# Opening, gate-weight loads and last output of a four-layer conditioned residual kernel, re-ordered

## The chip, the cores and the metric

The kernel runs on one core of a Trainium2 chip. The core's engines work side by side, each through its own queue in order: TensorE (PE in the profile, with PEld its weight loads), VectorE (DVE), ScalarE (ACT), GpSimd (POOL) and SyncE (SP), which here issues nearly all DMAs. Time is device microseconds of one whole execution, the median of several runs. One further execution was taken with the hardware profiler; its rows are what is read below.

## The reference, cut to what matters

`x` is 16 sequences (batch B) of 512 steps (S) with 512 features (D), all float32; `cond` is one vector of 512 per sequence. Four layers follow one another, each added to its input.

```
# layer 0: a wavelet transform, scaled by a gate and undone: as a whole v + gate * v
gate = sigmoid(silu(cond @ W1.T + b1) @ W2.T + b2)
x1 = x + (x + gate * x)                        # = x * (2 + gate)
# layer 1: a recurrence over the 512 steps, h0 = cond
h[t] = tanh(x1[t] @ Wx + b + h[t-1] @ Wh)
x2 = x1 + h
# layer 2: gates, then sums and products along the sequence
f, i = sigmoid(x2 @ Wf.T + bf), sigmoid(x2 @ Wi.T + bi)
f, i = f / (f + i + eps), i / (f + i + eps)
hidden = scan(f, i * (x2 @ Wh2.T + bh), start=cond)
x3 = x2 + hidden
# layer 3: a weight matrix of its own for each sequence
h3 = gelu(layernorm(cond) @ w1 + b1)
A, C = split(h3 @ w2 + b2)                     # 512 x 8 each, per sequence
out = x3 + x3 + x3 @ (base + A @ C.T)
```

## The kernel before

`P` is 128, `KC` is 4 (chunks of 128 features), `T` is 8 steps in a block, `NBLK` is 64 blocks, `BP` is 32.

**Opening (lines 208 to 297).** SP issues, in this order, `cond`, `condT` (the conditioning with features on partitions), `vecs` (bias vectors), `w1`, `w2`, `x0`, `wx`, `wh`, `x1` and a third block of x. ACT issues four small DMAs that spread the recurrence's bias over the partitions of `bias_sb`. POOL clears tiles, copies `condT` into `h0` (the start of the recurrence) and builds an identity. DVE and ACT normalize `cond` into `xhat`. `turned_layer` (L254) is a small dense layer: 16 products (32 passes of TensorE, since a float32 product takes two) into one PSUM bank, a 32x32 block transpose on DVE, a bias sum and a sigmoid. It runs twice, with `w1` and then `w2`, and yields `g2`, 2 + gate. `gated` (L167) multiplies a quarter of a block of x by `g2`; after the second layer DVE does the four quarters of block 0 and then the four of block 1.

**Recurrence (lines 299 to 577).** PE, ACT, DVE and SP follow the written order (`manual_schedule`). PSUM banks start as the bias (`begin`, L185: [...]ACT copies the bias in). `inputs(n, i, pre)` (L383) adds products of x1 with a chunk of `wx` to a bank; `accumulate` (L373) is the product itself, at L374 for `wx` and `wh` alike. A step then adds h @ Wh (16 products), ACT takes tanh in four pieces (L538), and DVE turns each piece (L539) into the operand of the next step. What else PE does in the wait for tanh is given per step: `inputs` of the next block (`SHARE`), a quarter of a layer of layer 3 (`layer_part`, L320), a quarter of an early gate of layer 2 (`early_gate`, L402, matmul at L421). In block 0, the first four `inputs` come ahead of the loop and those of the next step behind each step's h @ Wh. `end_layer(0)` (L344), at the end of block 0, takes the one Gelu (L358). Sigmoids of `early_gate` (L435) begin in block 4.

`wf`, `wi`, `wc` and `base`, 16 pieces of 256 KB, are loaded two at a time after each block from block 1 on (L563). `load_chunk` (L311) brings layer 3's weights through three buffers, and x comes a block at a time, into one buffer (`load_x`, L150).

**Gates and output (lines 579 to 681).** For each of 16 sequences, `gate_unit` (L588) does the rest of layer 2 for each of four feature chunks, and `last_layer` (L653) the output: for each of four groups of 128 steps, four products over k (L658) into one PSUM tile, a copy on ACT (L662) to `osb`, a tile of the pool `work`, which has two buffers, and a DMA out (L663). For the last sequence this starts when the previous one's is through; chunk 3 of its x3 is the last thing that DVE makes (L630).

```
    pending = None
    for b in range(B):
        ...
            if j == (KC - 1 if end else 1) and pending is not None:
                last_layer(*pending)
        ...
        pending = b, x3, base_sb if end else layer
    last_layer(*pending)
```

Of the kernel before, what the change touches and what calls it, by code (L numbers as in the profile page):

```python
# [70 lines left out]

EPS = 1e-8
# [7 lines left out]
def kernel(  # L80
# [127 lines left out]
    with tc.tile_pool(name="pre", bufs=1, side="right") as pre, tc.tile_pool(  # L208
        name="ps_pre", bufs=1, space=PSUM
    ) as ps_pre:  # L210
# [4 lines left out]
        nc.sync.dma_start(out=condT_sb, in_=chunks(condT))  # L215
        nc.sync.dma_start(out=vec_sb, in_=vecs)
        nc.sync.dma_start(out=w1_sb, in_=chunks(w1T))
        nc.sync.dma_start(out=w2_sb, in_=chunks(w2T))
        x0 = load_x(0, pre, "x0")
        nc.sync.dma_start(out=wx_sb, in_=chunks(wx))  # L220
        nc.sync.dma_start(out=wh_sb, in_=chunks(wh))
        x1 = load_x(1, pre, "x1")
        xb = load_x(2)
        for j in range(KC):
            nc.scalar.dma_start(
                out=bias_sb[j * BP : (j + 1) * BP],
                in_=l1b[:, j * BP : (j + 1) * BP]
                .rearrange("(o c) f -> o c f", o=1)
                .to_broadcast([BP, KC, BP]),
            )  # L230

        blank = pre.tile([P, 2 * P], BF16)
        nc.gpsimd.memset(blank, 0.0)
        nc.gpsimd.memset(h0, 0.0)
        nc.gpsimd.tensor_copy(h0[:, :, B : 2 * B], condT_sb)
        make_identity(nc, ident)
        for tile_ in (aeT, hT3, b2a_raw, *h_out[G - 2 : T - 1]):
            nc.gpsimd.memset(tile_, 0.0)

        stats = pre.tile([B, 6], F32)  # L240
# [11 lines left out]
        banks = [[begin(n, i, blank) for i in range(NBANK)] for n in range(2)]  # L252
# [22 lines left out]
        turned = ps_pre.tile([P, KC, B], F32, tag="ae", name="ae")  # L275

        def turn():
            for k in range(KC):
                nc.tensor.transpose(turned[:, k, :], xhat[:, k * P : (k + 1) * P], ident[:B, :B])

        def scale():
            for k in range(KC):
                nc.vector.tensor_scalar(
                    aeT[:, k, :B], turned[:, k, :], col(C_LNG, k), col(C_LNB, k), ALU.mult, ALU.add
                )

        z, gate = turned_layer(lambda k: h0[:, k, B:], w1_sb, C_L0B1, "hq", turn)
        hq = pre.tile([P, KC, BP], F32)
        nc.vector.tensor_tensor(hq, z, gate, ALU.mult)
        _, gate = turned_layer(lambda k: hq[:, k, :], w2_sb, C_L0B2, "g", scale)  # L290
# [4 lines left out]
        for i in range(len(MOVES)):  # L295
            gated(nc.vector, xs[1], x1, i)
# [443 lines left out]
```

## Time and profile before

| what | value |
|---|---|
| time, median of 3 runs (lowest, highest) | 1635.35 us (1634.92, 1636.69) |
| profiled execution, its own time | 1637.08 us |
| its span, first to last instruction | 1635.3 us |
| granted TensorE clock over the span | 0.999 |
| PE / DVE / ACT / POOL busy | 98% / 69% / 26% / 11% |
| first product of layer 0 (L259) | at 8.08 us |
| first tanh (L538) | at 19.28 us |
| first matmul of `gate_unit` (L594) | at 918.35 us |
| last copy of the output (L662) | at 1631.67 us |

The profile gives for each group of instructions its busy time, the mean duration of one, and the idle time of its engine ahead of it, with the instruction or DMA that ended that idle time. A timeline shows a start, a duration, the engine, the source line, the output and inputs, and in brackets the idle time before. SPq and ACTq are DMA issues of those queues. Matmul ends are modelled, so what counts for PE is the distance from start to start. The span and the time of the profiled execution differ by 1.8 us of launch and end.

### The profile page before, as it was taken

The numbers are of one execution on the slowest core, as the hardware profiler recorded it, in microseconds if no ns is written. First come the engines' busy times: TensorE is split into PE (matmuls) and PEld (weight loads), VectorE is DVE, ScalarE is ACT, GpSimd is POOL, SyncE is SP. The second block draws the span as 40 slices with busy tenths as digits, with TensorE's granted clock in tenths as the row PEclk, the third lists the DMA queues.
The fourth block names the chain that finished last, engine by engine and source line by source line (L and its number), as shares of the span: only waits on it lengthen the run. The fifth ranks groups of instructions, "written<-read, shape, count | busy, mean of one in ns | idle before, by whom it ended". The sixth has DMA issues, their size and how long they took to land.

```text
span 1635.3 us, 67511 instructions
## 1 busy us (share of the span) xinstructions
PE 1609.0 (98%) x29213; PEld 1142.2 (70%) x29213; DVE 1132.4 (69%) x3608; ACT 419.5 (26%) x2478; POOL 172.5 (11%) x144
## 2 busy tenths in 40 slices
PE   7999999999999999999999999999999999999998
PEld 6887888888888888888888655555555555555554
DVE  3445655656565656565655698888888888899886
ACT  3333333333333333333333211111111111111111
POOL 0000000000000000000000032222222222222221
PEclk9999999999999999999999999999999999999999
DMA  5445332111111111111110001111111111101111
GB/s 188 139 133 148 108 109 63 36 37 36 36 36 37 36 36 36 37 37 36 36 36 24 23 26 34 41 42 39 42 39 42 44 44 45 39 30 44 45 37 58
DMA packets 110171, 87.12 MB, mean 53 GB/s; under 512 B 19200, under 2 KB 88352, under 8 KB 109872
## 3 DMA queue, kind: packets, MB, share of 16 engines
q1 hardware_dynamic: 108768, 82.71, 16.8%
q8 instruction: 229, 3.75, 1.0%
q14 instruction: 70, 0.57, 0.1%
q10 hardware_dynamic: 1104, 0.08, 0.0%
HBM read 55.48 MB, written 27.28 MB: 51 GB/s over the span
## 4 chain that ended last, share of the span: by engine, by line
PE 91%; DVE 5%; issue 2%; DMA 1%; ACT 1%; POOL 0%; SPq 0%; DVEq 0%; POOLq 0%; ACTq 0%
PE pre L374 41%; PE po L658 12%; PE pg L421 12%; PE pf L594 8%; PE pi L594 8%; PE pc L594 8%; DVE s L611 1%; PE pl L648 1%; PE pf L334 1%; DVE s L623 1%; DVE s L619 1%; DVE i L622 0%; DMA w_sb<-in_w1T_dram 0%; DMA xb<-in_xT_dram 0%; DVE f L625 0%
## 5 line engine op out<-in xcount | busy, mean ns | idle before, releaser
L374 PEld LDWEIGHTS pre<-wh_sb,h_out 128*32 128x32 f32 x16384 | 461.6, 110 | 152.6 <-DVE h_out L539 148.1
L374 PE MATMUL pre<-wh_sb,h_out 128*32 128x128 f32 x16384 | 553.5, 273 | 5.1 <-DVE h_out L539 2.2
L539 DVE STREAM_TRANSPOSE h_out<-a 128x32 f32<-128x32 f32 x2048 | 264.5, 186 | 358.6 <-ACT a L538 358.0
L538 ACT ACTIVATE a<-pre 128x32 f32<-128x32 f32 x2048 | 238.2, 202 | 586.5 <-PE pre L374 586.5
L374 PE MATMUL pre<-wx_sb,x 128*32 128x128 f32 x8192 | 283.1, 274 | 2.8 <-DVE x L171 2.1
L374 PEld LDWEIGHTS pre<-wx_sb,x 128*32 128x32 f32 x8192 | 235.9, 110 | 4.1 <-issue 4.0
L658 PE MATMUL po<-layer,x 128*128 128x512 f32 x480 | 208.7, 592 | 0.5 <-POOL x L630 0.5
L594 PE MATMUL pf<-x,wf_sb 128*128 128x384 f32 (+2 forms) x512 | 168.9, 473 | 2.3 <-DVE x L544 1.3
L658 PEld LDWEIGHTS po<-layer,x 128*128 128x128 f32 x480 | 91.1, 190 | 111.6 <-issue 106.0
L594 PE MATMUL pc<-x,wc_sb 128*128 128x384 f32 (+2 forms) x512 | 165.3, 466 | 0.0
L594 PE MATMUL pi<-x,wi_sb 128*128 128x384 f32 (+2 forms) x512 | 165.3, 466 | 0.0
L611 DVE RECIPROCAL s<-s 128x384 f32<-128x384 f32 (+1 forms) x64 | 153.7, 2402 | 2.1
L594 PEld LDWEIGHTS pf<-x,wf_sb 128*128 128x128 f32 x512 | 96.7, 192 | 72.7 <-issue 18.5
L629 POOL TENSOR_TENSOR s<-s,f 128x512 f32<-128x512 f32 x63 | 86.4, 1371 | 513.5 <-DVE s L623 513.5
L594 PEld LDWEIGHTS pi<-x,wi_sb 128*128 128x128 f32 x512 | 97.3, 190 | 57.7 <-issue 0.2
L594 PEld LDWEIGHTS pc<-x,wc_sb 128*128 128x128 f32 x512 | 97.3, 190 | 57.6
L544 DVE TENSOR_TENSOR x<-x,h_out 128x128 f32<-128x128 f32 x256 | 101.1, 395 | 18.6
L609 ACT ACTIVATE f<-pf,vec_sb 128x384 f32<-128x384 f32 (+1 forms) x64 | 36.0, 562 | 289.2 <-POOL s L629 164.9
L662 ACT COPY osb<-po 128x512 f32<-128x512 f32 x64 | 37.5, 586 | 265.7 <-DMA out_dram<-osb 115.6
L610 DVE SCALAR_TENSOR_TENSOR s<-f,i 128x384 f32<-128x384 f32 (+1 forms) x64 | 35.1, 548 | 89.9 <-ACT i L609 88.8
L582 POOL MEMSET zero<- 128x1 f32 x1 | 0.1, 99 | 919.7 <-DMA early<-ei 919.7
L630 POOL TENSOR_TENSOR x<-s,x 128x512 f32<-128x512 f32 x63 | 83.2, 1320 | 4.9
(84 smaller groups left out, 1218.9 us busy)
## 6 DMA issues: line engine op xcount, KB each, us to landing
w<-in_l3w_dram SPq DMA_DIRECT2D x68, 256.0 KB
xb<-in_xT_dram SPq DMA_DIRECT2D x64, 256.0 KB
out_dram<-osb SPq DMA_DIRECT2D x64, 256.0 KB
early<-ef SPq DMA_DIRECT2D x19, 256.0 KB
early<-ei SPq DMA_DIRECT2D x19, 256.0 KB
f<-early SPq DMA_DIRECT2D x32, 64.0 KB
i<-early SPq DMA_DIRECT2D x32, 64.0 KB
f<-early SPq DMA_DIRECT2D x16, 96.0 KB
```

The source lines that it names most:

```text
L374: nc.tensor.matmul(pre[PLACE[g][0]][j * BP : (j + 1) * BP, PLACE[g][1], :], lhsT, tile_columns(w, j), start=False, stop=False, skip_group_ ...
L421: nc.tensor.matmul(ps[c * BP : (c + 1) * BP, :].rearrange("p (b t) -> p b t", **shape), w[:, k, j * P + c * BP : j * P + (c + 1) * BP], x2 ...
L538: nc.scalar.activation(a[:, at], pre[bank][:, place, at], AF.Tanh)
L539: nc.vector.transpose(turned[:, c, :], a[:, at])
L544: nc.vector.tensor_tensor(x2[:, :, :, at].rearrange("p k b t -> p k t b"), xs[n][:, :, t0 // 2, :, :], turned.rearrange("p k (t b) -> p k ...
L594: nc.tensor.matmul(p[:, te:], w_sb[:, k, j * P : (j + 1) * P], x2[:, k, b, te:], start=(k == 0), stop=(k == KC - 1),)
L609: nc.scalar.activation(gate[:, new], p[:, new], AF.Sigmoid, bias=col(bias, j))
L611: nc.vector.reciprocal(s[:, new], s[:, new])
L629: engine.tensor_tensor(s, s, f, ALU.add)
L630: engine.tensor_tensor(x3[:, j, :], s, x2[:, j, b, :], ALU.add)
L658: nc.tensor.matmul(po, x3[:, k, at], layer[:, k, :], start=(k == 0), stop=(k == KC - 1))
L662: nc.scalar.copy(osb, po)
```

## The change

Five things change.

1. The opening. `w1` is issued second on SP, right behind `cond`; `vecs` goes to ACT's queue. `condT` no longer feeds `h0`: TensorE turns `cond` (`turn`, four transposes) and DVE copies the result; `condT` itself is loaded later. The bias is loaded as one row of 2 KB; POOL multiplies it with the identity into `bias_rows`, four products with ones spread it over partitions, and ACT copies it to `bias_sb`. `idle_products(n)` issues n products of zeros, 512 columns wide: three at the start, four ahead of the first layer, one ahead of the second. The banks' zero products move from the start to between the two layers. `wh` is loaded ahead of `wx`, each in four pieces.
2. Block 0. The first h @ Wh stands ahead of the first `inputs`, whose two groups now follow it. The four quarters of block 1's gating move from ahead of the loop into steps 0 to 3. The pool `pre` is closed, and `x2` made, after step 3. The load of `b2a` moves from ACT's queue to SP's, and `condT` comes behind it.
3. A one-element sigmoid follows the Gelu in `end_layer(0)`.
4. The gate weights are loaded one piece at a time, after steps 1 and 5 of blocks 0 to 7.
5. The last sequence's output: chunks 0 to 2 of all four groups first, into four PSUM tiles, then chunk 3 of each with its copy and DMA.

In the instruction streams of the two programs, TensorE has eight more idle products, four more transposes and four bias products. In the changed one ACT's table load ahead of the Gelu waits for DVE, and the Gelu itself for POOL; before, the load waited for nothing and the Gelu for DVE. A second table load follows the Gelu, and the one ahead of the first early sigmoid is gone. ACT's last four copies wait for the DMA of two copies earlier, as before.

```diff
+IDLE = (3, 4, 1)
...
         nc.sync.dma_start(out=cond_sb, in_=cond)
-        nc.sync.dma_start(out=condT_sb, in_=chunks(condT))
-        nc.sync.dma_start(out=vec_sb, in_=vecs)
         nc.sync.dma_start(out=w1_sb, in_=chunks(w1T))
+        nc.scalar.dma_start(out=vec_sb, in_=vecs)
+        bias_row = pre.tile([KC, P], F32)
+        nc.scalar.dma_start(out=bias_row, in_=l1b)
         nc.sync.dma_start(out=w2_sb, in_=chunks(w2T))
         x0 = load_x(0, pre, "x0")
-        nc.sync.dma_start(out=wx_sb, in_=chunks(wx))
-        nc.sync.dma_start(out=wh_sb, in_=chunks(wh))
+        for k in range(KC):
+            nc.sync.dma_start(out=wh_sb[:, k, :], in_=wh[k * P : (k + 1) * P, :])
+        for k in range(KC):
+            nc.sync.dma_start(out=wx_sb[:, k, :], in_=wx[k * P : (k + 1) * P, :])
...
-        for j in range(KC):
-            nc.scalar.dma_start(
-                out=bias_sb[j * BP : (j + 1) * BP],
...
-        blank = pre.tile([P, 2 * P], BF16)
+        blank = pre.tile([P, D], BF16)
         nc.gpsimd.memset(blank, 0.0)
+        make_identity(nc, ident)
         nc.gpsimd.memset(h0, 0.0)
-        nc.gpsimd.tensor_copy(h0[:, :, B : 2 * B], condT_sb)
-        make_identity(nc, ident)
+        ones = pre.tile([KC, BP], F32)
+        nc.gpsimd.memset(ones, 1.0)
+        bias_rows = pre.tile([KC, KC, P], F32)
+        nc.gpsimd.tensor_tensor(
+            bias_rows,
+            bias_row.unsqueeze(1).to_broadcast([KC, KC, P]),
+            ident[:KC, :KC].unsqueeze(2).to_broadcast([KC, KC, P]),
+            ALU.mult,
+        )
...
+        def idle_products(n):
+            ps = ps_pre.tile([P, D], F32, tag="pre", name="idle")
+            for _ in range(n):
+                nc.tensor.matmul(ps, blank[:, :P], blank, start=True, stop=True)
+
+        def turn(src, name):
+            turned = ps_pre.tile([P, KC, B], F32, tag="ae", name=name)
+            for k in range(KC):
+                nc.tensor.transpose(turned[:, k, :], src[:, k * P : (k + 1) * P], ident[:B, :B])
+            return turned
+
+        idle_products(IDLE[0])
+        nc.vector.tensor_copy(h0[:, :, B : 2 * B], turn(cond_sb, "cond_turned"))
...
-        banks = [[begin(n, i, blank) for i in range(NBANK)] for n in range(2)]
+        bias_ps = ps_pre.tile([P, KC, BP], F32, tag="ae", name="bias")
+        for j in range(KC):
+            at = slice(j * BP, (j + 1) * BP)
+            nc.tensor.matmul(
+                bias_ps[at], ones, bias_rows[:, :, at], start=True, stop=True, skip_group_check=True
+            )
+        nc.scalar.copy(bias_sb, bias_ps)
...
-        z, gate = turned_layer(lambda k: h0[:, k, B:], w1_sb, C_L0B1, "hq", turn)
+        idle_products(IDLE[1])
+        z, gate = turned_layer(lambda k: h0[:, k, B:], w1_sb, C_L0B1, "hq", turn_xhat)
         hq = pre.tile([P, KC, BP], F32)
         nc.vector.tensor_tensor(hq, z, gate, ALU.mult)
+        banks = [[begin(n, i, blank) for i in range(NBANK)] for n in range(2)]
+        idle_products(IDLE[2])
         _, gate = turned_layer(lambda k: hq[:, k, :], w2_sb, C_L0B2, "g", scale)
...
-        for i in range(len(MOVES)):
-            gated(nc.vector, xs[1], x1, i)
-        nc.scalar.dma_start(out=b2a_raw[:, :, :R], in_=b2a)
...
             nc.scalar.activation(hT3[:, :, :B], z[:, :, :B], AF.Gelu)
+            nc.scalar.activation(z[:, 0, :1], z[:, 0, :1], AF.Sigmoid)
...
     pre, nxt = banks
-    for i in range(KC):
-        inputs(0, i, pre)
     for _ in range(AHEAD):
         load_chunk()
+    nc.sync.dma_start(out=b2a_raw[:, :, :R], in_=b2a)
+    nc.sync.dma_start(out=condT_sb, in_=chunks(condT))
...
             if n == 0 and s < G - 1:
-                for k in range(KC):
-                    inputs(0, (s + 1) * KC + k, pre)
+                for i in range((s + (s > 0)) * KC, (s + 2) * KC):
+                    inputs(0, i, pre)
...
+            if n == 0 and s < G:
+                gated(nc.vector, xs[1], x1, (0, 2, 1, 3)[s])
+            if n == 0 and s == G - 1:
+                opening.close()
+                x2pool = ctx.enter_context(tc.tile_pool(name="x2pool", bufs=1, side="right"))
+                x2 = x2pool.tile([P, KC, B, S], F32)
...
+            if s in (1, 5) and n < 2 * KC:
+                which, k = divmod(2 * n + s // 5, KC)
+                w_sb, w = ((wf_sb, wfT), (wi_sb, wiT), (wc_sb, wcT), (base_sb, base))[which]
+                nc.sync.dma_start(out=w_sb[:, k, :], in_=w[k * P : (k + 1) * P, :])
...
-        for i in (2 * n - 2, 2 * n - 1):
-            if 0 <= i < 4 * KC:
...
-        pending = b, x3, base_sb if end else layer
-    last_layer(*pending)
+        pending = b, x3, layer
+
+    pos = [
+        pool.tile([P, D], F32, tag=tag, name=f"po_{B - 1}_{t}", bufs=2)
+        for t, (pool, tag) in enumerate(((ps_g, "pl"), (ps_g, "pl"), (ps_o, "po"), (ps_o, "po")))
+    ]
+    for t, po in enumerate(pos):
+        output_part(po, t, x3, base_sb, range(KC - 1))
+    for t, po in enumerate(pos):
+        output_part(po, t, x3, base_sb, (KC - 1,))
+        leave(B - 1, t, po)
```

`output_part` issues the products of a group over the chunks it is given, and `leave` the copy to `osb` and the DMA out; together they are the body of the loop of `last_layer`.

## The prediction

> **What bounds the kernel now.** I read the page's busy times first, then the waits, then the chain and the timeline of the places that the diff touches.
>
> ```profile
> PE 1609.0 (98%) x29213; PEld 1142.2 (70%) x29213; DVE 1132.4 (69%) x3608; ACT 419.5 (26%) x2478; POOL 172.5 (11%) x144
> ...
> PEclk9999999999999999999999999999999999999999
> ```
>
> PE is busy 1609 of 1635.3 us, and the change removes no product of it (it adds a few). So what can be won is PE's 26 us of idle time and time in which its products run slowly. PE's waits in the first 60 us, then from 60 to 960 us:
>
> ```profile
> PE ps_hq L259 <- DMA w_sb<-in_w1T_dram: 5.9, 1, 5.9
> PE pre L374 <- DVE x L171: 2.1, 1, 2.1
> PE pre L192 <- POOL blank L233: 1.1, 1, 1.1
> PE ps_g L259 <- DVE hq L289: 0.9, 1, 0.9
> ...
> PE pg L421 <- DMA wc_sb<-in_wcT_dram: 1.7, 1, 1.7
> ```
>
> The opening holds 10 us of the 26, led by w1; one late gate weight holds 1.7 us more. The timeline of PE and of ACT in the opening:
>
> ```profile
> 15.52 1.93 PE L374 MATMUL pre<-wx_sb,x 128*32 128x128 f32 x32 [2.10 <-DVE x L171]
> 17.20 1.96 PE L374 MATMUL pre<-wh_sb,h_out 128*32 128x128 f32 x32
> 18.91 1.96 PE L374 MATMUL pre<-wx_sb,x 128*32 128x128 f32 x32
> 20.61 1.19 PE L374 MATMUL pre<-wh_sb,h_out 128*32 128x128 f32 x32
> ...
> 23.39 1.07 PE L374 MATMUL pre<-wx_sb,x 128*32 128x128 f32 x32
> 24.26 0.96 PE L374 MATMUL pre<-wh_sb,h_out 128*32 128x128 f32 x28
> ...
> 19.28 0.47 ACT L538 ACTIVATE a<-pre 128x32 f32<-128x32 f32 x4 [4.82 <-PE pre L374]
> 21.92 0.47 ACT L538 ACTIVATE a<-pre 128x32 f32<-128x32 f32 x4 [2.18 <-PE pre L374]
> 23.64 0.47 ACT L538 ACTIVATE a<-pre 128x32 f32<-128x32 f32 x4 [1.25 <-PE pre L374]
> ```
>
> From 17.20 to 18.91 32 passes take 1.71 us, 53 ns each; from 23.39 to 24.26 the same 32 take 0.87, 27 ns each. The granted clock reads 1.00 in both, so the slow state shows only in these distances. It ends near 20.7, after 5.2 us of unbroken work; every product of the two small layers ran in it. A step takes 2.64 us slow (19.28 to 21.92), 1.72 fast.
>
> Two places in the recurrence, seen on ACT, and the end, on ACT and PE:
>
> ```profile
> 33.07 1.28 ACT L358 ACT_TABLE_LOAD   x1
> 34.36 0.26 ACT L358 ACTIVATE hT<-got 128x64 f32<-128x64 f32 x1
> 34.52 0.44 ACT L538 ACTIVATE a<-pre 128x32 f32<-128x32 f32 x4
> ...
> 92.74 1.28 ACT L435 ACT_TABLE_LOAD   x1
> 94.04 0.69 ACT L435 ACTIVATE ef<-pg,vec_sb 128x512 f32<-128x512 f32 x1
> 94.62 0.45 ACT L538 ACTIVATE a<-pre 128x32 f32<-128x32 f32 x4
> ...
> 1620.17 11.43 PE L658 MATMUL po<-base_sb,x 128*128 128x512 f32 x26 [0.45 <-DVE x L630]
> 1631.67 0.59 ACT L662 COPY osb<-po 128x512 f32<-128x512 f32 x1 [2.85 <-PE po L658]
> ```
>
> Both table loads stand ahead of a tanh that the next step waits for.
>
> **The change part by part.** Step A, *the opening*, to the tanh of step 1, now at 21.92. Two paths meet there.
>
> The DMA path. Up to the last piece of wx four weights of 1.05 MB, x0 of 0.26 and 0.05 small must come, 4.51 MB. From 4.5 to 19.5 us the windows show 383 GB/s: 11.8 us. When does the flow begin? In before w1 is issued at 2.18 and the full rate starts at 4.5, 2.3 us later, with about 1,200 small packets (condT, the spread bias, vecs) at 57 to 109 GB/s ahead. The last output, with nothing ahead, is issued at 1632.28 and moves data from 1633.1, 0.85 us later. w1 is now issued at 1.18 with fewer than 200 small packets beside it: the flow starts between 2.0 and 3.5; I take 2.4, nearer the empty queue. w1 lands at about 5.5, wx at 14.2 plus 0.3 for the completion (the last output's data ends at 1634.0, SP sees it at 1634.27): 14.5. The later pieces of wx wait on SP for DMAs eight places earlier (w1, w2, x0); those land at 5.5 to 9, more than 2 us before their turn comes, so I cost this at 0; without that cover it is up to 2 us.
>
> The engines' path. Zeros from 1.2; cond lands at 2.58 as before; four transposes take 0.60 (the row of the four of xhat), the copy 0.2. bias_row, ACT's second issue (0.48 each), lands near 3.1 (cond took 1.84); POOL's multiply over 512 elements costs 1.37 by its row in the gate stage, so 4.5; four bias products 0.5; the four zero products, N = 512 at the slow rate, about 0.43 each (estimate, from the 427 ns of the Trainium skill, "TensorE: Matmul & The Clock Gate", Part 1; L658's f32 pass of 512 columns is 0.43 at full rate, two bf16 passes' worth), 1.7. So the first layer starts at 6.8, not at w1's landing. It takes 1.94 slow: 8.75. hq follows 1.46 later in before (10.02 to 11.48), but PE now has four transposes (0.60), 24 blank products (1.05) and one zero product (0.43) in between, 2.1: the second layer starts at 10.8. By then PE has worked without a hole of note since 4.5, 6.3 us, over the 5.2 that were enough: fast, 1.1, to 11.9. The gate and three quarters of gating take 2.08 (13.44 to 15.52): 14.0. The first h @ Wh lies in that wait, hidden while wh lands by 11.7.
>
> So the paths end at 14.5 and 14.0. The last k's wx products need 0.2 and their latency 0.2: first tanh at 14.9, the second one fast step of 1.75 later at 16.65, against 21.92: **5.2 us** gained. From both sides: flow at 2.0 gives 5.7. If PE stays slow throughout, 10.8 + 1.94 + 2.08 + 1.94 is 16.75, the next tanh 2.64 later at 19.4: 2.5 gained.
>
> Step B, *the sigmoid behind the Gelu*, in the hole between blocks 0 and 1. In before the load starts at 33.07, ahead of Gelu's operand (DVE's add at L357 ends at 33.79). In the changed stream the load itself waits for DVE, since the Gelu now waits for POOL: 33.8 to 35.1, Gelu to 35.4, the second load to 36.7, the one-element sigmoid 0.2 (the row of the 16x1 Sqrt): tanh at 36.85, not 34.52. **2.3 us** lost; behind that tanh wait four transposes and all of PE. The Trainium skill speaks against this edit: "ScalarE: Activation LUTs", What ACT_TABLE_LOAD costs, gives 1.28 us of load and about 1.38 of drain for each switch. The rows of before have the 1.28 and no drain: Gelu starts 0.01 us after its load. I take the rows; by the rule the new load costs 1.4 more, which I keep as the end of the range.
>
> Step C, *the first early sigmoid*. Without its load the sigmoid would run from 92.74 to 93.43, before the products of its step end at 93.7, so tanh at 94.62 moves to 93.75: **0.85 us** gained.
>
> Step D, *gate weights sooner*. PE waits at 126.33 for a piece issued at 122.92. Tanh to tanh there is 3.64 us (124.70 to 128.34), 1.75 in the next step: **1.9 us** gained, as that piece is now issued in step 1 of block 5, over ten steps ahead. The issues cost SP 0.45 each; SP's queue spends 15 us of the first 60 waiting for PE, which hides them.
>
> Step E, *the last output*. PE now fills the hole before 1620.17 (0.6 us) with other chunks: its last pass ends at 1630.9, not 1631.6. But the four copies no longer come 3.43 us apart. Chunk 3 of the groups ends at 1628.3, 1629.15, 1630.0 and 1630.9. Copies 1 and 2 end at 1628.95 and 1629.8; a DMA takes 2.0 from issue to SP's seeing it land, and osb has two buffers, so copy 3 waits to 1631.0 and copy 4 for the second DMA, to 1631.85: 0.2 later than 1631.67. **0.2 us** lost; from 0.7 gained (no wait) to 0.5 lost.
>
> Costed at nothing: block 1's gating in steps 0 to 3, four times 0.25 on DVE, which idles 0.9 us and more before each set of transposes (x1 and the third block land at 15.2 and 15.9, as DVE reaches them; up to 0.5 if late); condT and b2a in small packets, about 2 us of DMA time ahead of the x that was issued at 26.42 for use at 35.15.
>
> Sum: 5.2 - 2.3 + 0.85 + 1.9 - 0.2 = 5.45. The profiled execution took 1637.08, 1.7 above the median of 1635.35; I take the gain off the median: 1629.9, said as 1630.0.
>
> **The rivals.** *PE stays slow through the opening.* Zeros come in bursts of 1.3 and 1.7 us with holes of over 1 us while POOL makes the bias. For it: in before PE worked 8.08 to 10.6 and 11.48 to 13.4 and stayed slow. Against it: 6.3 us nearly unbroken. Then A is 2.5, the sum 2.75: 1632.6.
>
> *The hole of step B slows PE again.* PE's filler ends at 34.4 and h comes near 37.3, a hole of 2.9 us. The same page, Why this matters for your kernels, wants no holes over about 3 us. The trace has only one of 1.6 us (at 87.6) after which PE stays fast, so it can't decide. It would cost two or three slow steps, 0.9 each, 1.8 to 2.7: about 1632.2.
>
> *SP falls behind, and the kernel is slower.* A gate weight now stands ahead of each block's x in SP's queue, in blocks 1 to 7. x, issued at 40.49, is first used at 48.70 and takes 2.0 to land, 6.2 us in hand. If queued weights hold it over 7.0 us longer, DVE's queue, and with it the recurrence, loses 0.8 in each of seven blocks, which eats 5.45; at 8 us it is 1.8 a block, 12.6: 1642.5. For it: SP's queue is in order with its waits on earlier DMAs. Against it: the total of bytes in these blocks hardly changes, 256 KB per 7 us.
>
> **How the numbers follow.** The sum as worked out, with one end or other of its terms: 0.62, 1628.4 to 1631.4. Slow PE in the opening: 0.15. The hole: 0.10. Both of these at once, about 1634: 0.05. The slower rival, or a wait like it: 0.08. The instruction-issue stall of 1.6 us at 87.6 may move either way. Range 1628.1 to 1633.8. 0.2%, about what a measurement of this kernel can tell from no change, is 3.3 us: faster takes the likeliest case and part of the two rivals around 1632.4, 0.70; within 0.2% the rest of them, 0.22; slower 0.08.
>
> **What would show it.** First tanh near 14.9, the second 1.75 later; 27 ns a pass in the second layer's products; two table loads between 28 and 32 and a tanh 2.3 us later than the load-free order would give; no load near 90; no wait for wc; the last copies waiting for the output's DMA, the last one about 3.5 us from the end. A first tanh past 16, slow passes after block 0, or DVE waiting for xb would prove me wrong.

## The result and the profile after

The changed kernel took 1634.58 us (median of 14 runs, 1632.68 to 1638.50) beside 1636.74 us for the kernel before in the same comparison (14 runs, 1634.92 to 1639.18): ratio 0.9988, 95% interval 0.9979 to 0.9996. A second comparison (e13 below, 22 runs) gave 1635.37 us, ratio 0.9994, 0.9988 to 1.0001. So the change brings 1 to 2 us, some 0.1%, where 5.4 were forecast: within the 0.2% that counts as no change, and 0.8 us above the range. Its profiled execution took 1635.84 us with a span of 1634.1, against 1637.08 and 1635.3 before.

PE is what the page shows first, now busy 99% instead of 98%, but 4.7 us longer in sum:

```profile
PE 1613.7 (99%) x29233; PEld 1143.2 (70%) x29233; DVE 1133.1 (69%) x3609; ACT 419.9 (26%) x2480; POOL 173.5 (11%) x145
```

The 20 products added (zeros, the turned cond, the bias) take 5.2 us by their rows, so the rest of PE's work is hardly shorter. PE's waits in the first 60 us:

```profile
PE pre L400 <- DVE h_out L565: 2.9, 1, 2.9
...
PE pre L400 <- DVE x L173: 1.0, 1, 1.0
PE ps_hq L287 <- DMA w_sb<-in_w1T_dram: 0.7, 1, 0.7
```

The 5.9 us for w1 have become 0.7. On top stands a wait of 2.9 us for `h_out` (0.6 in the kernel before): the hole behind block 0, a stretch in which PE stands idle while ACT loads two tables. PE in the opening, and the tanhs of ACT:

```profile
7.18 1.94 PE L287 MATMUL ps_hq<-w_sb,h_out 128*32 128x128 f32 x32 [0.72 <-DMA w_sb<-in_w1T_dram]
...
11.22 1.94 PE L287 MATMUL ps_g<-w_sb,hq 128*32 128x128 f32 x32
12.93 1.32 PE L400 MATMUL pre<-wh_sb,h_out 128*32 128x128 f32 x32
15.23 1.95 PE L400 MATMUL pre<-wx_sb,x 128*32 128x128 f32 x64 [0.98 <-DVE x L173]
```

```profile
16.44 0.47 ACT L564 ACTIVATE a<-pre 128x32 f32<-128x32 f32 x4 [2.22 <-PE pre L400]
18.61 0.47 ACT L564 ACTIVATE a<-pre 128x32 f32<-128x32 f32 x4 [1.70 <-PE pre L400]
```

The second layer still takes 1.94 us, 53 ns a pass; only from 13.48, where the record of the clock begins, does PE run at 27. The wx products start when DVE has x ready, at 15.23; for wx itself PE does not wait here. The tanh of step 1 comes at 18.61 instead of 21.92: 3.3 us gained, and a stall of 0.5 in block 0 leaves 2.84 at its last tanh (29.34 against 32.18).

The end of block 0 on ACT, one line of the kernel before and then the changed kernel:

```profile
32.18 0.47 ACT L538 ACTIVATE a<-pre 128x32 f32<-128x32 f32 x4 [1.25 <-PE pre L374]
```

```profile
31.02 1.28 ACT L382 ACT_TABLE_LOAD   x1 [0.81 <-DVE got L381]
32.31 0.26 ACT L382 ACTIVATE hT<-got 128x64 f32<-128x64 f32 x1
32.59 1.28 ACT L384 ACT_TABLE_LOAD   x1
33.88 0.20 ACT L384 ACTIVATE got<-got 128x1 f32<-128x1 f32 x1
33.99 0.44 ACT L564 ACTIVATE a<-pre 128x32 f32<-128x32 f32 x4
...
36.47 0.47 ACT L564 ACTIVATE a<-pre 128x32 f32<-128x32 f32 x4 [1.87 <-PE pre L400]
38.54 0.47 ACT L564 ACTIVATE a<-pre 128x32 f32<-128x32 f32 x4 [1.61 <-PE pre L400]
```

From the last tanh of block 0 to the first of block 1 (the boundary, below) it takes 4.65 us, 2.34 before (32.18 to 34.52): 2.31 lost. The next two steps take 2.48 and 2.07 instead of 1.63 and 1.65, another 1.27 lost. Busy times by stretch (after each engine's count the column PEclk is the granted clock) say why:

```profile
30.00:34.00 4.00, 1.57 (x58) 1.30 (x48) 0.88 (x4) 3.15 (x6) 0.00 (x0) 1.00 0.47 147
34.00:37.40 3.40, 2.93 (x56) 2.67 (x60) 1.33 (x10) 1.06 (x10) 0.00 (x0) 0.50 0.04 10
37.40:41.00 3.60, 3.60 (x132) 3.24 (x128) 1.34 (x10) 1.10 (x9) 0.00 (x0) 1.00 0.47 146
```

The clock is halved for 3.41 us (33.96 to 37.38) right behind the hole; PE gets 56 products done in it, and 132 in the next 3.6 us.

Further on, the first early sigmoid gives 0.42 back, and in block 7 the wait for wc is gone (1.91). A stall of PE's issue at 87.6, 1.6 us in the profile before, does not occur (about 1.9); others of 0.5 to 1.2 us fall on other steps. The last tanh of the recurrence comes 3.76 us earlier (913.32 against 917.08). Of that 1.2 reach the end of the span. ACT at the last output:

```profile
1626.78 0.59 ACT L687 COPY osb<-po 128x512 f32<-128x512 f32 x1 [10.57 <-PE po L692]
1627.64 0.58 ACT L687 COPY osb<-po 128x512 f32<-128x512 f32 x1 [0.27 <-PE po L692]
1629.51 0.58 ACT L687 COPY osb<-po 128x512 f32<-128x512 f32 x1 [1.29 <-DMA out_dram<-osb]
1630.36 0.58 ACT L687 COPY osb<-po 128x512 f32<-128x512 f32 x1 [0.27 <-DMA out_dram<-osb]
```

The first two copies wait for PE, the last two for the output's DMA. And in the gate stage there is one more stretch at half clock. Before had it too, but for 3.41 us (from 1573.92), while it now lasts 6.83 (from 1569.96). Before, then after:

```profile
1566.80:1573.60 6.80, 5.42 (x18) 2.38 (x16) 6.76 (x9) 0.55 (x1) 2.04 (x2) 1.00 0.00 0
1573.60:1580.00 6.40, 6.40 (x18) 4.24 (x18) 6.40 (x10) 0.53 (x2) 0.66 (x1) 0.73 0.13 33
```

```profile
1566.80:1573.60 6.80, 4.92 (x11) 2.43 (x10) 6.76 (x10) 0.00 (x0) 2.69 (x2) 0.73 0.11 31
1573.60:1580.00 6.40, 6.40 (x19) 4.30 (x18) 6.40 (x10) 1.05 (x2) 0.79 (x1) 0.75 0.00 1
```

### The profile page after: what moved, and what is told of

Same layout as the page of the kernel before. It is cut to its first block, busy times and chain, and to the rows that moved or that the text cites. A ratio compares the mean times of both kernels' runs of the same rounds, so it can differ in the third digit from the quotient of the medians.

```text
span 1634.1 us, 67569 instructions
## 1 busy us (share of the span) xinstructions
PE 1613.7 (99%) x29233; PEld 1143.2 (70%) x29233; DVE 1133.1 (69%) x3609; ACT 419.9 (26%) x2480; POOL 173.5 (11%) x145
## 4 chain that ended last, share of the span: by engine, by line
PE 95%; DVE 2%; issue 1%; ACT 0%; DMA 0%; POOL 0%; SPq 0%; ACTq 0%; POOLq 0%; DVEq 0%
PE pre L400 41%; PE po L692 13%; PE pg L447 12%; PE pf L626 9%; PE pi L626 9%; PE pc L626 9%; PE pl L680 1%; PE pf L358 1%; DVE s L643 0%; DVE s L655 0%; DMA w_sb<-in_w1T_dram 0%; DVE s L651 0%; POOL x L662 0%; POOL s L661 0%; DVE h_out L565 0%
## 5 line engine op out<-in xcount | busy, mean ns | idle before, releaser
L687 ACT COPY osb<-po 128x512 f32<-128x512 f32 x64 | 37.5, 585 | 266.7 <-DMA out_dram<-osb 129.2
```

The source lines that it names most:

```text
L687: nc.scalar.copy(osb, po)
```

## The experiments

Each run was compared with runs of the kernel before on the same chip; a ratio below is to that. Nearly all differences are 1 to 4 us, and an interval of the median is 2 to 3 us wide. So the mechanism is read in the traces and the medians only say whether it reaches the end.

**The hole behind block 0.** Theory: the second load costs its own time, and the hole then halves the clock. *e1* is the changed kernel without the sigmoid:

```diff
-            nc.scalar.activation(z[:, 0, :1], z[:, 0, :1], AF.Sigmoid)
```

> The changed kernel without the one-element sigmoid behind the Gelu. Theory (the hole between blocks 0 and 1 lowers PE's clock): the second table load is gone, the first tanh of block 1 comes 1.5 us earlier after the last of block 0 (3.1 instead of 4.65 us), PE's hole shrinks from 2.9 to about 1.4 us, the granted clock stays 1.00 there, and the next two steps take 1.65 and 1.75 us instead of 2.48 and 2.07, 1.2 more. A load returns ahead of the first early sigmoid and costs 0.4 to 0.85. Net 1.9 to 2.3 us faster than the changed kernel: about 1632.5. Rival (the loads alone, the clock falls for another reason): the clock still falls, net 0.7 to 1.1 faster: about 1633.7.

Measured: 1633.98 us, ratio 0.9989 (0.9980 to 0.9997). The boundary takes 3.14 us (4.65 with the sigmoid), PE's hole is 1.4 instead of 2.9 us, and the clock stays at 1.00 through block 1. In the traces the sigmoid costs 1.51 at the boundary and 1.28 behind it, and returns 0.42. The median does not show those 2.4 us (the changed kernel's ratio is 0.9988); the same trace has a fall of the clock in the opening instead (14.93 to 18.34).

*e2* fills the hole with ten products of zeros in the first step of block 1 and leaves all else:

```diff
+            if n == 1 and s == 0:
+                ps = ps_q.tile([P, WIDE], F32, tag="pg", name="hole")
+                for _ in range(10):
+                    nc.tensor.matmul(ps, zeros_b[:, :P], zeros_b, start=True, stop=True)
```

> The changed kernel with ten products of zeros (N = 512) on PE in step 0 of block 1, where it waits for the Gelu, the two loads and the sigmoid. ACT's work there is the same. Theory (idle PE lowers its clock): the hole is under 1 us, the granted clock stays 1.00 there, tanh 0 to tanh 2 of block 1 takes 3.3 us instead of 4.55: 1.2 faster than the changed kernel, about 1633.4. Rival (the clock falls for another reason than PE's idling): it falls all the same, no gain.

Measured: 1634.98 us, ratio 0.9994 (0.9986 to 1.0003). The same stretches as above, of this kernel:

```profile
30.00:34.00 4.00, 3.78 (x69) 2.30 (x66) 0.98 (x5) 3.14 (x5) 0.00 (x0) 1.00 0.50 166
34.00:37.40 3.40, 2.82 (x100) 2.65 (x104) 1.33 (x10) 1.20 (x11) 0.00 (x0) 1.00 0.06 14
```

The boundary still takes 4.66 us, so ACT's wait is untouched; but the clock stays at 1.00, 100 products fit where 56 did, and the two steps are back at full speed (1.27 us). The median does not show it. So in this trace it is the hole that lets the clock fall, and the loads do so only through it. One trace is weak evidence, since the clock does not fall behind every such hole; the table in the point-by-point part counts all of them.

*e14* adds only the sigmoid to the kernel before.

```diff
             nc.scalar.activation(hT3[:, :, :B], z[:, :, :B], AF.Gelu)
+            nc.scalar.activation(z[:, 0, :1], z[:, 0, :1], AF.Sigmoid)
```

> Kernel before with only the one-element sigmoid behind the Gelu. Theory 1 (the wait and the slow steps after it): the tanh after block 0 comes 2.3 us later, the clock falls for one window behind the hole and two or three steps cost 1.3 together, the load near 92.7 is gone and gives 0.4 to 0.85 back: 2.7 to 3.2 us slower than before. Rival (in this kernel PE's filler reaches further into the hole, so no slow window): 1.5 to 1.9 slower, granted clock 1.00 throughout block 1.

Measured: 1636.34 us beside 1636.26, ratio 0.9996 (0.9988 to 1.0004). ACT at the boundary:

```profile
32.73 0.38 ACT L200 COPY pre<-bias_sb 128x256 f32<-128x256 f32 x1
33.12 1.28 ACT L358 ACT_TABLE_LOAD   x1
34.42 0.26 ACT L358 ACTIVATE hT<-got 128x64 f32<-128x64 f32 x1
34.69 1.28 ACT L360 ACT_TABLE_LOAD   x1
35.98 0.20 ACT L360 ACTIVATE got<-got 128x1 f32<-128x1 f32 x1
36.09 0.44 ACT L540 ACTIVATE a<-pre 128x32 f32<-128x32 f32 x4
```

Here the first load starts right behind the copy, with no wait for DVE. The boundary takes 3.86 us (1.51 more), PE's hole is 1.82 us, and the clock stays at 1.00 through block 1. The tanh at the first early sigmoid gains 0.80. The rival was right about the clock; of its 1.5 to 1.9 us about 0.7 are lost in the trace and nothing in the median. The 2.3 us of the changed kernel are thus 1.5 for the sigmoid and 0.8 because the Gelu's load waits for DVE there.

**The opening.** Two theories for the missing part of the gain: PE at half speed in the second layer, or wx landing later than forecast. *e4* puts the banks' zero products, which stand between the two layers, ahead of the first, so that they do not keep PE from the second:

```diff
-IDLE = (3, 4, 1)
+IDLE = (3, 4, 2)
...
         nc.scalar.copy(bias_sb, bias_ps)
+        banks = [[begin(n, i, blank) for i in range(NBANK)] for n in range(2)]
...
-        banks = [[begin(n, i, blank) for i in range(NBANK)] for n in range(2)]
```

> The changed kernel with the banks' zero products and bias copies ahead of the first small layer, not between the two layers, and two zero products instead of one ahead of the second layer. Theory (what stands between the layers on PE delays the second): the second layer starts 0.7 us earlier against the first one's start (3.3 us after it, not 4.04), first tanh 0.5 to 0.7 earlier; if PE gets fast before the second layer, since it works with fewer holes from 4 us on, 0.9 more. About 1633.5, to 1632.9. Rival (DMA sets the first tanh): wx comes last, the first tanh stays at 16.4.

Measured: 1634.83 us, ratio 0.9998 (0.9990 to 1.0006); neither theory nor rival came true, and the profiled execution, at 1639.78 us, was the slowest of its 13. The second layer runs fast at 11.01, but the first tanh comes at 17.85, 1.4 later than in the changed kernel: PE waits 1.46 us for a piece of wx, until 17.10, and the clock is halved from 17.18 on.

*e5* keeps PE busy through the whole opening with more zeros:

```diff
-IDLE = (3, 4, 1)
+IDLE = (3, 6, 1)
...
         nc.vector.tensor_copy(h0[:, :, B : 2 * B], turn(cond_sb, "cond_turned"))
+        idle_products(2)
...
+            if n == 0 and s == 0:
+                ps = ps_q.tile([P, WIDE], F32, tag="pg", name="fill")
+                for _ in range(4):
+                    nc.tensor.matmul(ps, blank[:, :P], blank, start=True, stop=True)
```

> The changed kernel with PE's holes in the opening filled by more products of zeros: two behind the transposes of cond, six instead of four ahead of the first layer, four between the first h @ Wh and the first wx products. Theory 1 (step A fell short because PE was slow in the second layer): that layer runs at 27 ns a pass, x1 of block 0 is ready near 13.5 and the first tanh comes near 14.9, 1.5 us earlier; no fall of the clock before 30 us. Theory 2 (the weights come later than I put it): x1 is ready as early, but PE then waits for wx, and the first tanh stays at 16.0 to 16.5; what the fill saves is only the slow windows that such waits bring, under 1 us. By 1: about 1633.0; by 2: 1634.0.

Measured: 1633.86 us, ratio 0.9993 (0.9984 to 1.0001). PE in its opening:

```profile
7.49 1.08 PE L288 MATMUL ps_hq<-w_sb,h_out 128*32 128x128 f32 x32
...
10.05 1.08 PE L288 MATMUL ps_g<-w_sb,hq 128*32 128x128 f32 x32 [0.25 <-DVE hq L318]
...
15.68 0.43 PE L401 MATMUL pre<-wx_sb,x 128*32 128x128 f32 x8 [0.71 <-DMA wx_sb<-in_wx_dram]
16.35 1.30 PE L401 MATMUL pre<-wx_sb,x 128*32 128x128 f32 x40 [0.25 <-DMA wx_sb<-in_wx_dram]
```

Both layers run at full speed, and the first tanh is no earlier for it: 16.91, as PE waits for wx until 16.35. That speaks for the transfers. *e6* is e5 without w2's transfer:

```diff
-        nc.sync.dma_start(out=w2_sb, in_=chunks(w2T))
...
-        _, gate = turned_layer(lambda k: hq[:, k, :], w2_sb, C_L0B2, "g", scale)
+        _, gate = turned_layer(lambda k: hq[:, k, :], w1_sb, C_L0B2, "g", scale)
```

> The kernel of the opening filled, with w2 left out: it isn't loaded, and the second small layer multiplies by w1. The same instructions on PE, 1.05 MB less in the queue ahead of x0, wh and wx. Theory 2 (DMA sets the first tanh): wx lands 2.7 us earlier (1.05 MB at 383 GB/s) and the first tanh comes 1.5 us or more earlier than with the opening filled alone, to where the path over the gates ends, near 14.5. Theory 1 (PE's rate and the gates set it): no change, under 0.3 us.

Measured: 1633.27 us, ratio 0.9981 (0.9974 to 0.9987). The wait for wx is gone, and the wx products start when DVE has gated x:

```profile
14.34 1.95 PE L399 MATMUL pre<-wx_sb,x 128*32 128x128 f32 x64 [0.22 <-DVE x L173]
```

First tanh at 15.55, 1.36 us earlier than in e5. So with PE at full speed the bytes ahead of wx set the first tanh. From the start of the wx products to the first tanh it takes 1.21 us here, as in the changed kernel (15.23 to 16.44).

*e12* is the opening alone: the changed kernel without the sigmoid and with the gate weights and the last output as before.

> Parts 1 and 2 of the change alone: the changed kernel without the sigmoid behind the Gelu, with the gate weights loaded after the blocks and the last output in its order as before. By the corrected step A the tanh of step 1 comes at 18.6 (3.3 us gained), and the Gelu's table load, which waits for DVE, gives 0.7 back: about 2.6 faster than before, 1633.3. By step A as predicted, 5.2 and 4.5: 1631.4.

Measured: 1633.53 us, ratio 0.9974 (0.9964 to 0.9983). First tanhs at 16.27 and 18.84; the boundary takes 3.14 us, so the load's wait for DVE comes with the opening. The last tanh of block 0 gains 2.41, and the first of block 1 keeps 1.6. The ratio is worth 4.2 us (interval 2.8 to 5.9; the medians differ by 3.6), more than these 1.6 and nearer to the 4.5 of step A as predicted. *e16* below, which adds the weights, gains less.

**Gate weights.** *e8* moves only the loads of the gate weights, in the kernel before.

```diff
+            if s in (1, 5) and n < 2 * KC:
+                which, k = divmod(2 * n + s // 5, KC)
...
-        for i in (2 * n - 2, 2 * n - 1):
-            if 0 <= i < 4 * KC:
```

> The kernel before with the gate weights alone loaded after steps 1 and 5 of blocks 0 to 7. By step D the wait for wc in block 7 is gone and the tanh there come 1.9 to 2.1 us earlier: about 1634 against 1636. Rival (SP's queue falls behind, x late): DVE waits for xb in blocks 1 to 7 and it is slower than before.

Measured: 1634.67 us, ratio 0.9989 (0.9980 to 0.9998). The tanh at (block 7, step 3) gains 1.91 us, DVE does not wait for `xb` between 20 and 160 us (2.4 us before), and the ratio is worth 1.8 us.

*e16* is the opening and the weights, without the sigmoid and with the old last output.

> Changed kernel without the early sigmoid and with the old last output: the new opening and the earlier gate weights alone. Theory 3 (the parts add up): 3.3 to 4.2 from the opening and 1.8 from the weights, 5 to 6 us under the kernel before, near 0.9965 of it. Rival (what the recurrence gains is lost again in the gate stage, where a slow window of TensorE grows from 3.4 to 6.8 us): 3 to 4 us under it, with the last tanh of the recurrence 5 us earlier and the span only 3 to 4 shorter.

Measured: 1632.82 us, ratio 0.9977 (0.9968 to 0.9986), 3.8 us. The rival was right in the main: the last tanh is 5.74 us earlier, the last reciprocal 5.3, the span 4.5. The clock is halved for 6.83 us in the gate stage (3.41 before), and from the last reciprocal to the last copy it takes 22.1 us (21.4 before).

**The last output and its buffers.** Theory: the new order bunches the four copies, and two `osb` buffers make them wait for the DMAs. *e10* is the kernel before with the new order, *e3* the changed kernel with a third buffer; *e7* and *e11* are the kernel before with a third buffer, with the old and the new order.

```diff
-        osb = work.tile([P, D], F32, tag="osb", name=f"osb_{b}_{t}")
+        osb = work.tile([P, D], F32, tag="osb", name=f"osb_{b}_{t}", bufs=3)
```

> The kernel before with the new order of the last output alone. Step E: from PE's first pass of the last sequence to the end of the span 18.4 to 18.7 us, against 18.3 before; copies 3 and 4 wait for DMAs; time as before within 0.5 us. Rival (PE's filled hole counts): 0.7 us faster.

> The changed kernel with three osb buffers instead of two. Theory (the last copies wait for a buffer, step E): copies 3 and 4 of the last sequence follow their products, 0.86 us apart, without a wait for a DMA; the last copy starts 14.0 us after the first pass of the last sequence instead of 15.0, the span ends about 1.0 us earlier: 1633.6. Rival (the four DMAs close together hold each other up): copies early, but the last DMA lands as late as now, under 0.3 gained.

> The kernel before with three osb buffers instead of two, nothing else. With the changed kernel the third buffer took 7.5 us off. If that comes from the gate stage, which both kernels share (the third and fourth copies of each sequence wait for a DMA that stands in SP's queue behind loads that wait for VectorE), it takes about as much off here: 1628.5 to 1630. If it came from the new order of the last output alone, no more than 1 us.

> The same with three osb buffers. Theory (the buffer, not the DMAs, held the new order back): the four last copies follow their products 0.86 us apart and the order is now worth 0.7 to 1.5 us over the kernel before with three buffers (1633.7): about 1632.5. Rival (three buffers and the new order have nothing to do with one another): 1633.7.

Measured: e10 1637.47 us, ratio 1.0001 (0.9992 to 1.0009); e3 1627.14, 0.9954 (0.9941 to 0.9966); e7 1633.69, 0.9988 (0.9979 to 0.9997); e11 1631.55, 0.9971 (0.9960 to 0.9982). With two buffers the order is worth nothing, with three about 2.8 us (0.9971 against 0.9988, though the two intervals overlap). For e7 neither forecast holds: its 2 us lie between the 1 and the 6 or more. For e3 both sides had expected 1 us at most. The last copies of e3:

```profile
1618.85 0.59 ACT L687 COPY osb<-po 128x512 f32<-128x512 f32 x1 [10.57 <-PE po L692]
1619.70 0.59 ACT L687 COPY osb<-po 128x512 f32<-128x512 f32 x1 [0.27 <-PE po L692]
1620.56 0.59 ACT L687 COPY osb<-po 128x512 f32<-128x512 f32 x1 [0.27 <-PE po L692]
1621.57 0.59 ACT L687 COPY osb<-po 128x512 f32<-128x512 f32 x1 [0.42 <-DMA out_dram<-osb]
```

They are 0.86 us apart, the fourth 1.0. From the last reciprocal to the last copy e3 takes 19.1 us, the changed kernel 23.3 and the kernel before 21.4; that is 4.2 us against the changed kernel. Another 3.2 us lie earlier in the gate stage (690.5 us from the last tanh to the last reciprocal against 693.75). ACT's waits there (total, times, longest), first of the changed kernel, then of e3:

```profile
ACT osb L687 <- DMA out_dram<-osb: 129.2, 24, 8.3
```

```profile
ACT osb L687 <- DMA out_dram<-osb: 0.4, 1, 0.4
```

With two buffers ACT stands 129 us before copies whose buffer is still going out, and the activations queue behind. With three it does not, PE's wait of 1.9 us for DVE near 1567 is gone, and the clock does not fall there (nor in e7, e9 and e11):

```profile
1566.80:1573.60 6.80, 6.80 (x27) 4.82 (x26) 6.80 (x11) 1.05 (x2) 0.00 (x0) 1.00 0.02 5
1573.60:1580.00 6.40, 6.40 (x25) 4.42 (x24) 6.33 (x9) 1.05 (x2) 2.67 (x2) 1.00 0.11 32
```

*e15* is the changed kernel with the old order, *e13* the changed kernel once more, on the same chip as e14 and e16.

> Changed kernel with the last output computed in the old order. Theory 2 (the new order costs 1 to 2 us when the slow window before it lasts 6.8 us, as the copies then wait for two output transfers): 1 to 2 us under the changed kernel of this call, last copies 3.4 us apart, from last reciprocal to last copy 21.4 to 22.3 us. Rival (the order is worth nothing with two buffers, as it was when it alone was added to the kernel before): within 0.5 us of the changed kernel.

> The changed kernel once more, beside three kernels that each hold some of its parts, so that all four are compared with the same runs of the kernel before. Theory (the parts add up: opening 3.3 to 4.2 gained, sigmoid 3.0 lost, weights 1.8 gained, last output about nothing): 2 to 3 us under the kernel before. Rival (slow windows of TensorE move by chance from run to run and the first comparison fell badly): 4 us or more under it.

Measured: e15 1634.34 us, ratio 0.9985 (0.9978 to 0.9992); e13 1635.37, 0.9994 (0.9988 to 1.0001). The new order costs about 1 us in the changed kernel, though the two intervals overlap; for e13, 1 us under the kernel before, neither forecast came true. On this one chip the ratios make a row: opening and weights 0.9977, with the sigmoid 0.9985, with the new order too 0.9994; only its two ends are apart beyond their intervals. The traces show when the order costs. From the last reciprocal to the last copy the old order takes 21.4 us when the late half-clock stretch lasts 3.41 us (before, e8, e15) and 22.1 to 22.3 when it lasts 6.83 (e12, e14, e16); the new order takes 21.6 (e2, e5) and 22.6 to 23.3 (after, e1, e4, e6, e10, e13). So it loses 0.2 in the one case, 0.3 to 1.2 in the other.

e13's trace shows one more thing. It is the same program as the changed kernel, and its opening ran otherwise:

```profile
10.20 1.08 PE L287 MATMUL ps_g<-w_sb,hq 128*32 128x128 f32 x32 [0.25 <-DVE hq L317]
...
13.77 0.43 PE L400 MATMUL pre<-wx_sb,x 128*32 128x128 f32 x8 [0.29 <-DMA wx_sb<-in_wx_dram]
15.79 3.53 PE L400 MATMUL pre<-wx_sb,x 128*32 128x128 f32 x56 [1.59 <-DMA wx_sb<-in_wx_dram]
```

PE was fast at 10.2, stood 1.59 us for wx, and the clock was halved from 15.07 to 21.90: tanhs at 17.73 and 21.15, and 0.3 us gained at the end of block 0, where the first profile had 2.84. It then passed the hole behind block 0 with the clock at 1.00. So from one execution to the next the half-clock stretches sit in different places.

**The best version.** *e9* is the changed kernel without the sigmoid, with three `osb` buffers, and with `hT3` cleared by DVE instead of POOL, so that the Gelu's load does not wait:

```diff
+        nc.vector.memset(hT3, 0.0)
-        for tile_ in (aeT, hT3, b2a_raw, *h_out[G - 2 : T - 1]):
+        for tile_ in (aeT, b2a_raw, *h_out[G - 2 : T - 1]):
```

> The changed kernel without the sigmoid behind the Gelu, with DVE clearing the Gelu's output tile in place of POOL (so that the table load needn't wait), and with three osb buffers. Theory: tanh 0 of block 1 comes 2.3 us after the last of block 0 as in the kernel before, PE's hole is under 1 us, its clock keeps up there; with the 7.5 us of the third buffer and 2.3 + 1.3 - 0.5 from the hole: about 1624.5. Rival (the third buffer's 7.5 was chance of few runs): 1629 or more.

Measured: 1627.47 us, ratio 0.9944 (0.9930 to 0.9958), about 9 us under the kernel before. The boundary takes 2.36 us and the clock is at 1.00 from 12.9 to 1620.6. It beats both kernels; from e3 (0.9954) the intervals do not separate it. It lies between the theory's 1624.5 and the rival's 1629.

## Why the prediction was wrong, point by point

The step that failed is step A, the size of the gain in the opening: 5.2 us were forecast, and 2.4 to 2.8 were left at the end of block 0, because both of the paths that were to end at 14.5 and 14.0 us ended more than 1 us later. The second miss, 1.27 us, is a fall of the clock that the sum left out as an unlikely rival.

- **Step A, 5.2 us forecast: 3.3 at the tanh of step 1, 2.4 to 2.8 at the end of block 0** (after and six other profiles with this opening: e1, e2, e3, e12, e15, e16), 0.3 in e13. The DMA path was sized with full rate from 2.4 and wx landed at 14.5. The stretches of the changed kernel (last column: GB/s) show the start:

```profile
1.50:2.50 1.00, 1.00 (x3) 0.15 (x1) 0.00 (x0) 0.71 (x1) 0.59 (x4) 1.00 0.41 72
2.50:3.50 1.00, 0.81 (x5) 0.50 (x4) 0.08 (x1) 0.57 (x1) 0.59 (x1) 1.00 0.80 195
3.50:4.50 1.00, 0.51 (x8) 0.20 (x8) 0.93 (x4) 0.00 (x0) 1.00 (x5) 1.00 0.97 328
4.50:5.50 1.00, 1.00 (x7) 0.38 (x4) 0.70 (x3) 0.83 (x3) 0.72 (x4) 1.00 1.00 342
```

  The rate climbs from 1.5 to 4.0 us rather than starting at 2.4, and by 7.5 us 1.65 MB have moved instead of 1.95: 0.8 us late. And bytes moved are not bytes landed: w1 was seen at 7.15 when 1.5 MB had moved, of which w1 and what was ahead of it are 1.1; the 4.51 MB up to wx had moved by 14.9, and its last piece landed at 15.62 in this profile, and was seen at 15.62 in e16, 16.35 in e5 and 17.10 in e4. So wx came 1.1 us later than forecast here, and up to 2.6 in others.

  The engines' path failed as well, and in the changed kernel's own profile it was the later one: PE waited for DVE's x until 15.23, not for wx. Of the 1.23 us over the forecast 14.0, w1 took 0.38 (it came at 7.15 instead of 5.5, so the first layer, due at 6.8 by the other work, started at 7.18) and the slow second layer 0.84 (1.94 instead of 1.1). That is the rival "PE stays slow through the opening", held at 0.15: in after, e2, e3 and e9 the second layer was slow, in e1, e12, e13, e15 and e16 fast. The forecast had PE fast by 10.8, after 6.3 us of work; here it rose at 13.48, 6.3 us after the first layer began, in e12, e15 and e16 at 10.5 to 11.0. And the sum was short by itself: it counted 0.4 us from the end of the later path to the first tanh, the last quarter of the wx products and their latency. But when x comes last all 32 stand behind it, 1.21 us as measured, so 14.0 would have given 15.2, not 14.9.

  The two delays do not add. With the second layer fast, PE waited for wx last, and the first tanh came at 16.0 to 16.4 (e1, e12, e15, e16; 17.73 in e13), against 16.44 in after; e5 shows that a fast PE alone gains nothing, e6 that with fewer bytes as well it gains 0.9 against after.
- **Step B, -2.3: measured -2.31**, with the load's wait for DVE (0.81), two loads of 1.28 and no drain between them: the Gelu starts 0.01 us after its load's end, the second load 0.02 after the Gelu. The trace's price was the right one; the drain of 1.38 that the Trainium skill gives ("ScalarE: Activation LUTs", What ACT_TABLE_LOAD costs) is in no row here.
- **The rival "the hole of step B slows PE again", held at 0.10 and 0.05, came true** in the profiled execution: 1.27 us on top, in two steps. e1 and e2 show it. It was not certain, though: with the same two loads there, e3 and e6 (hole 2.7 us) and e13 (2.9 us, the same program) ran block 1 at full clock; e4, e5 and e15 (2.9, 2.7, 2.7) did not. The rule of the Trainium skill ("TensorE: Matmul & The Clock Gate", Why this matters for your kernels: no holes over about 3 us) gives the size but no sharp limit: 2.9 us did it in one execution of the changed kernel and not in the other. What tells them apart in the traces is where the hole lies. All changes of the clock in one execution lie a whole number of 3.413 us apart (13.48, 33.96 and 37.38 in after; 8.25, 15.07 and 21.90 in e13), and this grid lies differently in each execution. PE's busy time in the unit of the grid that holds most of the hole:

| profile | hole | PE busy in that unit | clock behind it |
|---|---|---|---|
| e15, after, e5, e4 | 2.7, 2.9, 2.7, 2.9 us | 0.73, 1.02, 1.15, 1.20 us | 0.50 |
| e3, e6, e13 | 2.7, 2.7, 2.9 us | 1.57, 1.64, 1.96 us | 1.00 |
| e14 | 1.8 us | 1.59 us | 1.00 |
| e16, e12, e1 | 1.4, 1.3, 1.4 us | 2.02, 2.07, 2.17 us | 1.00 |

  The clock fell where PE was busy for 1.20 us of the 3.413 or less, and not from 1.57 on. e13's hole was split by the grid (1.96 and 1.97 us busy), after's lay in one unit. This is read off eleven traces, not tried by an experiment, and it holds for this place only: in the opening and the gate stage the clock also fell behind units in which PE was busy for longer.
- **Step C, +0.85: measured 0.4 to 0.80** (e13 0.38, after 0.42, e15 0.64, e14 0.80) and nothing in e2 and e6, where this step took 2.52 and 2.75 us without a load (2.53 with it) as PE's products came late. The load of 1.28 is gone; what the step gains differs by profile.
- **Step D, +1.9: measured 1.91, also alone.** The wait on wc is gone, and the slower rival did not come: from 20 to 160 us the changed kernel has no wait for `xb`, where before had 2.4 us of it.
- **Step E, -0.2: the mechanism as forecast**, two copies wait for PE and two for the DMA. The size holds with a short late half-clock stretch; with the long one it is -0.3 to -1.2.
- **Not in the prediction at all: the late half-clock stretch** at the second `make_layer`, where PE stands 1.9 us for DVE (1.4 before). With two buffers it lasts 3.41 us in five profiles and 6.83 in nine. With the longer one the way from the last reciprocal to the last copy takes 0.7 to 1.7 us more.

Added up as measured: 2.6 - 2.3 - 1.3 (in some executions) + 0.6 + 1.9, less 0.2 to 1.2, gives 0.3 to 2.6; the medians say 1 to 2. The timed runs carry no trace, but each has its mean granted clock, of which one stretch of 3.41 us at half clock is 0.001. With the old output order, on one chip, it averages 0.9984 for the kernel before (54 runs), 0.9981 for e16 (10 runs) and 0.9974 for e15 (19 runs), which differs from e16 by the sigmoid. So the sigmoid seems to bring a stretch more in about two of three executions (an estimate, 0.0007 over 0.001), not in the profiled one alone. e1's runs have 0.9975, no more than the changed kernel's 0.9972 and 0.9975: without the sigmoid the clock seems to have been lost elsewhere, as its trace shows for the opening, which may be why its median did not move.

What stays open is where the stretches sit in the timed runs, what decides the late one, and why e12 gained more than its trace explains. Stalls of PE's issue differ by 2 us in sum between profiles without relation to the edits, about as much as the effects looked for: e10 and e7 have the recurrence of the kernel before, and their last tanhs come 1.24 and 1.71 us earlier than its own.

## What to carry to other kernels

Size a transfer path by the rate measured from its first byte, start-up included, and by when the consumer sees the data; count the younger traffic that moves with it (0.4 MB here). A hole in PE of nearly 3 us cost twice here, as a wait and, in some executions, as a half-clock stretch behind it, and a few products of zeros in it took the second part away at no cost to the first. When an edit bunches work, look for the buffer that will be the new wait: here one more 2 KB buffer per partition was worth three to six times the whole change.

## What the runs showed of the hardware that was not expected

The granted clock changes in units: the stretches at 0.50 inside the kernel are 3.413 or 6.827 us long in all the profiles, and all changes of one execution lie on one grid of 3.413 us. It falls after holes much shorter than 3 us too: 1.59 us behind eight products in e13, 1.89 us in the gate stage behind products over 8 rows. The 1.82 us of e14, behind products over all 128 rows, were not followed by one, nor were the 2.9 us of e13, which the grid divides.

The column of the granted clock reads 1.00 before its first recorded change, although the passes of 53 ns show half speed there; up to that change only the distance of the passes tells the rate.

With two output buffers ACT waited 115.6 us before (129.2 after) for output DMAs; PE, the busiest engine, shows of it a wait of 1.4 us for DVE before (1.9 after). A third buffer took 5.6 to 6.5 us off the changed kernel by the ratios (7.4 by the two traces) and 2 off the kernel before.
